# The source lists of a graph kernel: five long gathers and moves by powers of two in place of 49 short gathers

## The chip, the cores and the metric

The kernel runs on one core of a Trainium2 chip. A core has five engines with a queue of instructions each: TensorE (PE), VectorE (DVE), ScalarE (ACT), GpSimd (POOL) and SyncE (SP). Each engine executes its own instructions in the order in which they were issued and waits on semaphores for the others. SP, ACT and POOL also issue DMA transfers. The metric is the time of one execution on the device in microseconds; the median over several executions counts.

## The reference: what is computed

A graph has 6250 nodes with 256 features each and 100000 edges `src -> dst`, sorted by `dst`. Two blocks follow one another, each with a residual and a layer norm:

```python
x = _layernorm(x + _L0_gnn_ref(x, edge_index, Wl1, Wr1, att1, b1, Wl2, Wr2, att2, b2))
x = _layernorm(x + _L1_gnn_ref(x, W, a, src, dst))
```

The first block is two GATv2 layers with 4 heads of 64 channels. Each layer multiplies x by two weight matrices (`xl`, `xr`), and for each edge forms a logit from `leaky_relu(xl[src] + xr[dst])` and the attention vector, takes a softmax of the logits over all edges that end in one node, and adds up `xl[src]` with these weights. The second block is a GAT layer with 8 heads of 32 channels, with logits `s1[src] + s2[dst]`. So each layer needs, for every node, the list of the sources of its edges: a contiguous piece of the array `src`, as the edges are sorted by `dst`.

## The kernel before

The program has a plan (`make_plan`, L715), the three layers (`tile_by_degree`, L1143), and a general path (L81) that runs only if the plan finds that the graph doesn't fit its assumptions (`fits`, `done`).

**The layers.** The nodes are sorted by degree, largest first, and cut into 49 blocks (`NB`) of 128, one node to a partition. A block is worked on with as many columns as its largest node has edges (`cols`; the largest number is `CM` = 38). For each column POOL issues one indirect gather of 128 rows of the table (L1235). VectorE makes the logits (L1504 to L1506), ScalarE the softmax, and TensorE or VectorE adds up.

**The plan** makes what the layers need:

- `near_d`, a table in DRAM with a row for each node: up to 38 source numbers, the rest filled with the number of a node that doesn't exist, and then the node's 256 features;
- `node_i`, which node stands where in the order by degree;
- `xl1_d`, the table of `x @ Wl1` for the first layer, with the place of each node in one more column.

A node n stands at partition n % 128, column n // 128 in the plan's tiles before the change (`part`, L946 to L950). Its steps, in the order of the code:

1. VectorE finds in `dst` where each node's run of edges ends (L927 to L956), and TensorE adds one-hots of these runs into `count`, the degree of each node (L972).
2. Two matmuls give sums over a block's 128 partitions (`pc`, L980, L981); VectorE turns them into `begin_i`, the place in the list where each node's edges begin (L986 to L993).
3. POOL issues 49 indirect gathers (L998): each reads, for 128 nodes, the 38 numbers of the list from the beginning of the node's piece on, into `near`. The list is a copy of `src` in DRAM, `list_d`.
4. VectorE and TensorE work out the place of each node in the order by degree: one-hots `oh` of the degree (L1024), matmuls `pk` and scans into `cum` (L1033 to L1044), `place_f` (L1046); then one-hots `to_hi`, `given`, `to_lo` (L1071 to L1080) and 49 matmuls `pp` (L1085), from which come `node_i` and the check `wrong`, `fits` (L1091 to L1116).
5. `lacking` (L1004) marks in `no` which of a node's 38 columns lie behind its last edge; `fill` (L1011) puts the missing number there with a predicated copy and writes nine columns of nodes to `near_d` from SP's queue (L1016). There are six such spans.

Between these steps stands the making of the first table. `tables(n)` (L848) does the next n of 49 blocks: TensorE turns 128 rows of x (L834) and multiplies them (L843), ScalarE copies the result out of PSUM (L845), SP writes it to `xl1_d` (L846). The blocks are handed out by hand: 12 while VectorE looks for runs, then 1, 2 and 12 between the matmuls of step 4, and 22 behind `pp` (as 4, 7 and 11). The result tiles have ten buffers (`table1_row`). `pk` has two buffers in PSUM and its matmuls come in two groups of three.

The plan is written under `tc.manual_schedule()` (L691), so each engine gets its instructions in the order in which the code issues them. A second such part holds the layers. Between the two all engines read `fits` and branch (L700, L701). POOL begins the layers with small tiles (L1182) and the gathers of `near_d`'s rows for the first three blocks (`start1`, L1595).

Of the kernel before, what the change touches and what calls it, by code (L numbers as in the profile page):

```python
# [26 lines left out]
F32 = mybir.dt.float32  # L27
BF16 = mybir.dt.bfloat16
# [7 lines left out]
P = 128  # L36
# [678 lines left out]
def make_plan(  # L715
# [21 lines left out]

    one = ctx.enter_context(tc.tile_pool(name="plan_one", bufs=1))
# [7 lines left out]
    list_d = dram.tile([-(-E // CM) * CM + CM], I32, name="list_d")  # L746
# [124 lines left out]
    if rest:  # L871
# [9 lines left out]
    nothing = filled_tile("nothing", [1, list_d.shape[0] - E], 0, I32)  # L881
# [3 lines left out]
    nc.scalar.dma_start(list_d[E:].unsqueeze(0), nothing)  # L885
    nc.scalar.dma_start(
        list_d[:E].rearrange("(a b) -> a b", a=a), src.rearrange("(a b) -> a b", a=a)
# [4 lines left out]
    ranks = iota("ranks", [P, CM], [[1, CM]])  # L892
    ones = filled_tile("ones_f", [P, P], 1.0)
# [48 lines left out]
    for what in "lar":  # L942
# [4 lines left out]
    nc.vector.tensor_scalar(  # L947
        part[:, 0, :], run_i, SHIFT, P - 1, op0=OP.logical_shift_right, op1=OP.bitwise_and
    )
    nc.vector.tensor_single_scalar(part[:, 1, :], run_i, SHIFT + 7, op=OP.logical_shift_right)  # L950
# [27 lines left out]

    pc = ps.tile([P, 2, NB], F32, name="pc", tag="ph")
    nc.tensor.matmul(pc[:, 0, :], ones, count, start=True, stop=True)  # L980
    nc.tensor.matmul(pc[:, 1, :], above, count, start=True, stop=True)  # L981
# [3 lines left out]
    block = one.tile([P, NB], F32, name="block")  # L985
    nc.vector.tensor_copy(block, pc[:, 0, :])  # L986
    upto = one.tile([P, NB], F32, name="upto")
    nc.vector.tensor_tensor_scan(upto, ones_k[:, :NB], block, 0.0, op0=OP.mult, op1=OP.add)
    from_f = one.tile([P, NB], F32, name="from_f")
    nc.vector.tensor_sub(from_f, upto, block)  # L990
    nc.vector.tensor_add(from_f, from_f, pc[:, 1, :])
    begin_i = one.tile([P, NB], I32, name="begin_i")
    nc.vector.tensor_scalar(begin_i, from_f, float(E), 0.0, op0=OP.min, op1=OP.max)  # L993
    near = one.tile([P, NB, CM], I32, name="near")
    no = one.tile([P, NB, CM], I32, name="no")
    listed = list_d.rearrange("(a b) -> a b", b=CM)
    for k in range(NB):
        nc.gpsimd.indirect_dma_start(  # L998
            out=near[:, k, :], out_offset=None, in_=listed,
            in_offset=bass.IndirectOffsetOnAxis(ap=begin_i[:, k : k + 1], axis=1),  # L1000
        )
# [136 lines left out]
    for k in spans[4:]:  # L1138
        fill(*k)
# [653 lines left out]
```

## Time and profile before

| what | us |
| --- | --- |
| median of 14 runs (3367.95 to 3373.56) | 3370.39 |
| the profiled execution, its own time | 3369.12 |
| its span, first to last instruction | 3367.3 |
| VectorE busy | 2834.5 (84%) |
| POOL busy | 2464.9 (73%) |
| TensorE busy | 1340.3 (40%) |
| ScalarE busy | 1048.3 (31%) |
| POOL, 49 list gathers L998 | 59.3 |
| POOL, layers' gathers L1235, both tables | 2215.9 (1488.1 + 727.8) |

How to read it: the times of the profile are those of one execution, counted from its first instruction. A busy time is the sum over an engine's instructions; the share is of the span. A line such as `L998 POOL DMA_INDIRECT near<-list_d,begin_i x49 | 59.3, 1211 | 32.1 <-...` gives the line of the code, the engine, the operation, what is written from what, how often, the busy time in us, the mean of one in ns, and how long the engine stood idle just before, with what ended most of that. In a timeline the first two numbers are the start and the duration, and the brackets hold the idle time before and who ended it. An indirect DMA shown on POOL is the time that POOL takes to issue it; the data land later.

### The profile page before, as it was taken

The numbers are of one execution on the slowest core, as the hardware profiler recorded it, in microseconds if no ns is written. First come the engines' busy times: TensorE is split into PE (matmuls) and PEld (weight loads), VectorE is DVE, ScalarE is ACT, GpSimd is POOL, SyncE is SP. The second block draws the span as 40 slices with busy tenths as digits, with TensorE's granted clock in tenths as the row PEclk, the third lists the DMA queues.
The fourth block names the chain that finished last, engine by engine and source line by source line (L and its number), as shares of the span: only waits on it lengthen the run. The fifth ranks groups of instructions, "written<-read, shape, count | busy, mean of one in ns | idle before, by whom it ended". The sixth has DMA issues, their size and how long they took to land.

```text
span 3367.3 us, 23607 instructions
## 1 busy us (share of the span) xinstructions
PE 1340.3 (40%) x5129; PEld 1067.9 (32%) x5130; DVE 2834.5 (84%) x2648; ACT 1048.3 (31%) x4176; POOL 2464.9 (73%) x2613
## 2 busy tenths in 40 slices
PE   6346566666776753445455556563000000000000
PEld 5234445455555543434344444442000000000000
DVE  7289999999999988999999999995977676667666
ACT  3124444444445532444344444442000000000000
POOL 6677777777777777777777777657777777777776
PEclk8677888788888986777777777776555555555555
DMA  9644444444444444444444444434433333333333
GB/s 192 143 112 116 119 117 118 121 120 121 121 120 124 124 131 110 116 118 117 121 120 125 126 131 123 117 97 109 108 108 108 107 108 108 108 108 108 107 107 88
DMA packets 196123, 395.60 MB, mean 117 GB/s; under 512 B 63036, under 2 KB 115514, under 8 KB 195956
## 3 DMA queue, kind: packets, MB, share of 16 engines
q0 software_dynamic: 122048, 338.04, 38.1%
q1 hardware_dynamic: 66226, 54.22, 5.8%
q10 hardware_dynamic: 7698, 1.74, 0.5%
q8 instruction: 45, 0.74, 0.1%
q14 instruction: 106, 0.87, 0.1%
HBM read 353.82 MB, written 40.42 MB: 117 GB/s over the span
## 4 chain that ended last, share of the span: by engine, by line
DVE 30%; POOL 29%; issue 19%; PE 6%; DMA 5%; ACT 4%; DVEq 0%; POOLq 0%; ACTq 0%
POOL g L1235 28%; DVE z L1504 9%; DVE z L1505 8%; DVE lg L1506 8%; PE acc L1418 5%; DMA g<-xl_d,near_r 3%; ACT wt L1381 3%; DVE g L1411 2%; POOL out L1733 1%; DMA g<-whs_d,near_r 1%; DMA out<-y,node_i 1%; DVE weighted L1433 1%; DVE top L1374 1%; PE pm L1362 0%; ACT by L1388 0%
## 5 line engine op out<-in xcount | busy, mean ns | idle before, releaser
L1235 POOL DMA_INDIRECT g<-xl_d,near_r x1569 | 1488.1, 948 | 526.2 <-issue 434.0
L1418 PE MATMUL acc<-g,ident 128*128 128x256 f32 x3408 | 962.6, 452 | 777.3 <-DVE sd L1461 456.2
L1418 PEld LDWEIGHTS acc<-g,ident 128*128 128x128 f32 x3408 | 782.8, 233 | 957.9 <-issue 502.2
L1235 POOL DMA_INDIRECT g<-whs_d,near_r x766 | 727.8, 950 | 233.8 <-issue 227.2
L1504 DVE TENSOR_TENSOR z<-g,pr 128x1820 f32<-128x1820 f32 (+4 forms) x234 | 497.1, 2125 | 16.8 <-DMA g<-xl_d,near_r 8.9
L1505 DVE TENSOR_TENSOR z<-z,at 128x1820 f32<-128x1820 f32 (+4 forms) x234 | 497.5, 2126 | 8.0
L1506 DVE TENSOR_REDUCE lg<-z 128x28 f32<-128x1820 f32 (+4 forms) x234 | 497.3, 2125 | 8.1
L1410 ACT ACTIVATE g<-g,by 128x64 f32<-128x64 f32 x2056 | 500.0, 334 | 0.0
L1411 DVE TENSOR_TENSOR g<-g,wt 128x1792 f32<-128x1792 f32 (+8 forms) x234 | 348.3, 1505 | 2.8
L1442 DVE TENSOR_REDUCE acc_v<-weighted 128x256 f32<-128x4096 f32 (+15 forms) x49 | 343.7, 7014 | 1.7
L1391 ACT ACTIVATE wt<-lg 128x128 f32<-128x128 f32 (+17 forms) x49 | 14.0, 285 | 804.2 <-DVE lg L1390 804.2
L1381 ACT ACTIVATE wt<-lg,top 128x19 f32<-128x19 f32 (+14 forms) x392 | 115.3, 294 | 469.7 <-DVE top L1374 421.6
L1703 DVE TENSOR_TENSOR lg<-g,s_r 128x56 f32<-128x56 f32 (+4 forms) x111 | 22.3, 212 | 269.3 <-DMA g<-whs_d,near_r 215.1
L1433 DVE TENSOR_TENSOR weighted<-g,wt 128x1792 f32<-128x1792 f32 (+4 forms) x111 | 226.6, 2056 | 0.1
L1357 ACT COPY xT<-pt 128x256 f32<-128x256 f32 x147 | 55.0, 374 | 490.3 <-PE pt L1355 490.3
L1362 PE MATMUL pm<-wcat,xT 128*128 128x260 f32 x392 | 99.0, 395 | 22.6 <-ACT xT L1357 22.6
L1362 PEld LDWEIGHTS pm<-wcat,xT 128*128 128x128 f32 x392 | 70.4, 189 | 42.9 <-ACT xT L1357 34.3
L998 POOL DMA_INDIRECT near<-list_d,begin_i x49 | 59.3, 1211 | 32.1 <-DVE begin_i L993 17.4
L1381 ACT ACTIVATION_READ_ACCUMULATOR wt<-lg,top 128x1 f32 x392 | 73.1, 187 | 0.0
L1733 POOL DMA_INDIRECT out<-y,node_i x49 | 49.8, 1017 | 26.1 <-issue 14.2
L1362 PE MATMUL pm<-wh_cat,xT 128*128 128x272 f32 x196 | 59.0, 424 | 22.6 <-ACT xT L1357 22.6
L1362 PE MATMUL pl<-wcat,xT 128*128 128x260 f32 x196 | 57.0, 414 | 25.2 <-ACT xT L1357 25.2
(232 smaller groups left out, 1407.6 us busy)
## 6 DMA issues: line engine op xcount, KB each, us to landing
g<-xl_d,near_r POOLq DMA_INDIRECT x1569, 2.8
g<-whs_d,near_r POOLq DMA_INDIRECT x766, 2.8
whs_d<-row SPq DMA_DIRECT2D x49, 132.0 KB, 2.0
xl_d<-xl SPq DMA_DIRECT2D x49, 130.0 KB, 5.3
xl_d<-row SPq DMA_DIRECT2D x49, 130.0 KB, 2.5
xr_d<-row SPq DMA_DIRECT2D x49, 130.0 KB, 3.0
two<-xl_d SPq DMA_DIRECT2D x49, 130.0 KB, 3.3
two<-xr_d SPq DMA_DIRECT2D x49, 130.0 KB, 3.3
```

The lines of the kernel that those rows point to most:

```text
L1235: nc.gpsimd.indirect_dma_start(out=g[:, j + own - s0, :width], out_offset=None, in_=table, in_offset=source(of, b, j),)
L1362: nc.tensor.matmul(pm, xT[:, c, :], w[:, c, :], start=c == 0, stop=c == 1)
L1381: nc.scalar.activation(wt[:, :, h], lg[:, :S, h], AF.Exp, bias=top[:, h : h + 1], accum_out=den[:, h : h + 1],)
L1410: nc.scalar.mul(g4[:, t, h, :], g4[:, t, h, :], by[:, t - m, h : h + 1])
L1411: nc.vector.tensor_mul(g4[:, :m], g4[:, :m], wt[:, s0 : s0 + m, :].unsqueeze(3).to_broadcast([P, m, H, F // H]),)
L1418: nc.tensor.matmul(acc, ident, g4[:, t], start=s0 + t == 0, stop=s0 + t == S - 1 and not more)
L1433: nc.vector.tensor_mul(prod[:, s0 - base : s1 - base, :].rearrange("p t (h d) -> p t h d", h=H), g[:, :n, :F].rearrange("p t (h d) -> p t ...
L1442: nc.vector.reduce_sum(part, prod[:, : s1 - base, :].rearrange("p s f -> p f s"), axis=AX.X)
L1504: nc.vector.tensor_max(z, g[:, :n, :W2], xr[:, None, :].to_broadcast([P, n, W2]))
L1505: nc.vector.tensor_mul(z, z, at[:, None, :].to_broadcast([P, n, W2]))
L1506: nc.vector.reduce_sum(lg[:, s0:s1, :], z.rearrange("p t (h d) -> p t h d", h=H2), axis=AX.X)
L1733: put = nc.gpsimd.indirect_dma_start(out=out[:, :], out_offset=node(b), in_=y, in_offset=None, bounds_check=N - 1, oob_is_err=False,)
```

## The change

The plan counts its nodes partition by partition: node n now stands at partition n // 49 and column n % 49. So a partition's 49 nodes are neighbours in the sorted edge list, and their sources are one contiguous stretch of it. Each partition reads this stretch in five pieces of 309 numbers (`LONG`), one piece for ten nodes (`STEP`), by five gathers in place of 49. As a node has 16 edges on average (`MEAN`), the piece of node j of ten begins near number 16 j of the piece; how far off it begins (`off`, kept between 0 and 127 by a lead of 64) is known from a running sum over the partition. VectorE takes, for each j, 101 numbers of all five pieces into `moved`, from place 16 j, or from 64 further on where the highest of the seven bits of `off` is set (a copy and a predicated copy). Then it moves all 50 pieces by 32, 16, 8, 4, 2 and 1 numbers where the bit is set, by a predicated copy of the tile onto itself, and the first 38 numbers of each piece are the node's list.

With it go: `begin_i` now comes from sums over a row and a prefix over the partitions, so the two matmuls `pc` have one column; the division by 49 is a multiplication and a shift; `oh` and the bits stand on VectorE ahead of the moves, the scans `cum` behind them; all six `fill`s are issued together behind `lacking`, where two, one, one and two stood apart before; `near_d` and the place column of `xl1_d` are written in the other order; the check has a term more. The order of the `tables` calls is as before.

```diff
+    SEGS, STEP, BITS = 5, 10, 7
+    LEAD = 1 << BITS - 1
+    MEAN = E // N
+    LONG = MEAN * (STEP - 1) + CM + 2 * LEAD - 1
+    WIDE = CM + LEAD - 1
...
+    nc.scalar.dma_start(list_d[:LEAD].unsqueeze(0), nothing[:, :LEAD])
+    nc.scalar.dma_start(list_d[LEAD + E :].unsqueeze(0), nothing)
...
-    nc.vector.tensor_scalar(
-        part[:, 0, :], run_i, SHIFT, P - 1, op0=OP.logical_shift_right, op1=OP.bitwise_and
+    nc.vector.tensor_single_scalar(part[:, 1, :], run_i, SHIFT, op=OP.logical_shift_right)
+    nc.vector.tensor_single_scalar(part[:, 0, :], part[:, 1, :], float(by), op=OP.mult)
+    nc.vector.tensor_single_scalar(part[:, 0, :], part[:, 0, :], down, op=OP.logical_shift_right)
+    nc.vector.scalar_tensor_tensor(
+        part[:, 1, :], part[:, 0, :], -float(NB), part[:, 1, :], op0=OP.mult, op1=OP.add
     )
-    nc.vector.tensor_single_scalar(part[:, 1, :], run_i, SHIFT + 7, op=OP.logical_shift_right)
...
-    pc = ps.tile([P, 2, NB], F32, name="pc", tag="ph")
-    nc.tensor.matmul(pc[:, 0, :], ones, count, start=True, stop=True)
-    nc.tensor.matmul(pc[:, 1, :], above, count, start=True, stop=True)
+    total = one.tile([P, 1], F32, name="total")
+    nc.vector.reduce_sum(total, count, axis=AX.X)
+    pc = ps.tile([P, 2], F32, name="pc", tag="ph")
+    nc.tensor.matmul(pc[:, 1:], above, total, start=True, stop=True)
+    nc.tensor.matmul(pc[:, :1], ones, total, start=True, stop=True)
+    upto = one.tile([P, NB], F32, name="upto")
+    nc.vector.tensor_tensor_scan(upto, ones_k[:, :NB], count, 0.0, op0=OP.mult, op1=OP.add)
...
+    begin_i = one.tile([P, SEGS], I32, name="begin_i")
+    nc.vector.tensor_scalar(begin_i, begin_f, float(E), 0.0, op0=OP.min, op1=OP.max)
+    piece_of = one.tile([P, SEGS, LONG], I32, name="piece_of")
+    listed = list_d.rearrange("(a b) -> a b", b=LONG)
+    for k in range(SEGS):
+        nc.gpsimd.indirect_dma_start(
+            out=piece_of[:, k, :], out_offset=None, in_=listed,
+            in_offset=bass.IndirectOffsetOnAxis(ap=begin_i[:, k : k + 1], axis=1),
+        )
...
+    oh = one.tile([P, KEYS, NB], BF16, name="oh")
+    nc.vector.tensor_tensor(
+        oh, steps, key[:, None, :].to_broadcast([P, KEYS, NB]), op=OP.is_equal
+    )
...
+    off_i = one.tile([P, SEGS, STEP], I32, name="off_i")
+    nc.vector.tensor_scalar(off_i, off, 0.0, float(2 * LEAD - 1), op0=OP.max, op1=OP.min)
+    bit = one.tile([P, BITS, SEGS, STEP], I32, name="bit")
+    for k in range(BITS):
+        nc.vector.tensor_scalar(
+            bit[:, k], off_i, k, 1, op0=OP.logical_shift_right, op1=OP.bitwise_and
+        )
+    moved = one.tile([P, SEGS, STEP, WIDE], I32, name="moved")
+    for k in range(STEP):
+        for first_at in (0, LEAD):
+            data = piece_of[:, :, MEAN * k + first_at : MEAN * k + first_at + WIDE]
+            if first_at == 0:
+                nc.vector.tensor_copy(moved[:, :, k, :], data)
+            else:
+                nc.vector.copy_predicated(
+                    moved[:, :, k, :],
+                    bit[:, BITS - 1, :, k : k + 1].to_broadcast([P, SEGS, WIDE]), data,
+                )
+    every = moved.rearrange("p s j w -> p (s j) w")
+    bits = bit.rearrange("p b s j -> p b (s j)")
+    for k in range(BITS - 2, -1, -1):
+        n = CM + (1 << k) - 1
+        nc.vector.copy_predicated(
+            every[:, :, :n], bits[:, k, :].unsqueeze(2).to_broadcast([P, SEGS * STEP, n]),
+            every[:, :, 1 << k : (1 << k) + n],
+        )
+    near = every[:, :NB, :CM]
...
-    for k in range(NB):
-        nc.gpsimd.indirect_dma_start(
-            out=near[:, k, :], out_offset=None, in_=listed,
-            in_offset=bass.IndirectOffsetOnAxis(ap=begin_i[:, k : k + 1], axis=1),
-        )
...
-            near_d[k0 * P : k1 * P, :CM].rearrange("(k p) c -> p k c", p=P).bitcast(I32),
+            near_d.rearrange("(p k) c -> p k c", k=NB)[:, k0:k1, :CM].bitcast(I32),
...
     tables(1)
-    oh = one.tile([P, KEYS, NB], BF16, name="oh")
...
-            xl1_d[:NP, W2:].rearrange("(b p) w -> p b w", p=P), place_f.unsqueeze(2)
+            xl1_d[:NP, W2:].rearrange("(p b) w -> p b w", b=NB), place_f.unsqueeze(2)
...
     for k in spans:
         lacking(*k)
-    fill(*spans[0])
-    fill(*spans[1])
+    for k in spans:
+        fill(*k)
...
-        node_i, got[:, 1, :], float(P), got[:, 0, :], op0=OP.mult, op1=OP.add
+        node_i, got[:, 0, :], float(NB), got[:, 1, :], op0=OP.mult, op1=OP.add
...
-    fill(*spans[2])
...
     tables(7)
-    fill(*spans[3])
...
     tables(NB)
-    for k in spans[4:]:
-        fill(*k)
```

## The prediction

> **What bounds the kernel now.** I read the page first, for where the changed code lies. All of it is in `make_plan`, before the three attention layers. The later part, 3237 of the 3367 us, is not edited: POOL issues one gather every 1.25 us there and VectorE is nearly always busy. So the question is by how much the first gather of that part moves.
>
> ```profile
> span 3367.3 us, 23607 instructions
> ...
> L998 POOL DMA_INDIRECT near<-list_d,begin_i x49 | 59.3, 1211 | 32.1 <-DVE begin_i L993 17.4
> ...
> L1235 POOL DMA_INDIRECT g<-xl_d,near_r x1569 | 1488.1, 948 | 526.2 <-issue 434.0
> ```
>
> Second, the timeline of POOL over the plan: the 49 list gathers run from 40.2 to 114.3 us, and the first gather of the layers starts at 130.6.
>
> ```profile
> 40.23 1.36 POOL L998 DMA_INDIRECT near<-list_d,begin_i  x1 [17.41 <-DVE begin_i L993]
> 41.89 0.95 POOL L998 DMA_INDIRECT near<-list_d,begin_i  x1 [0.30 <-issue]
> ...
> 113.33 0.94 POOL L998 DMA_INDIRECT near<-list_d,begin_i  x1 [0.30 <-issue]
> 129.82 0.24 POOL L1182 IOTA numbers<- 128x128 f32 x1 [15.54 <-DMA near_d<-near]
> 130.02 0.12 POOL L1186 IOTA own_number<- 128x1 f32 x1
> 130.10 0.19 POOL L1200 MEMSET ones_l<- 128x128 f32 x1
> 130.59 0.97 POOL L1595 DMA_INDIRECT near_r<-near_d,node_i  x1 [0.30 <-issue]
> ```
>
> Third, the waits between 70 and 131 us (engine, line, what it waited for: us in total, times, longest). VectorE waits 38.4 us for list gathers, so it has room there. But ScalarE, which copies the table blocks out of PSUM, also waits: 14.3 us for table writes.
>
> ```profile
> DVE near L1013 <- DMA near<-list_d,begin_i: 38.4, 5, 15.5
> POOL numbers L1182 <- DMA near_d<-near: 15.5, 1, 15.5
> ACT xl L845 <- DMA xl_d<-xl: 14.3, 5, 8.4
> ACT xT L836 <- PE pt L834: 13.7, 1, 13.7
> ```
>
> Fourth, the timelines of VectorE, TensorE and ScalarE. They show a second chain as long as POOL's: scans, one-hots, `pp`, then 22 table blocks, the last of which is copied out at 117.4 us, as late as the last fill.
>
> ```profile
> 39.85 0.72 DVE L1024 TENSOR_TENSOR oh<-steps_k,key_b 128x1078 bf16<-128x1078 bf16 x1
> 41.13 1.22 DVE L1034 TENSOR_TENSOR_SCAN cum<-ones_k,pk 128x512 f32<-128x512 f32 x1 [0.55 <-PE pk L1033]
> ...
> 61.39 6.68 DVE L1080 TENSOR_TENSOR to_lo<-each_lo,to 128x6272 bf16<-128x6272 bf16 x1
> ...
> 116.31 0.55 DVE L1013 COPY_PREDICATED near<-no,far 128x342 int32<-128x342 int32 x1 [15.47 <-DMA near<-list_d,begin_i]
> 117.12 0.33 DVE L1013 COPY_PREDICATED near<-no,far 128x152 int32<-128x152 int32 x1 [0.25 <-DMA near<-list_d,begin_i]
> ```
> ```profile
> 42.40 0.18 PE L1033 MATMUL pk<-oh,ones_b 128*128 128x54 bf16 x1 [1.31 <-DVE cum L1034]
> ...
> 68.13 4.99 PE L1085 MATMUL pp<-given,to_lo 128*128 128x147 bf16 x49 [8.85 <-DVE to_lo L1080]
> ```
> ```profile
> 116.98 0.38 ACT L845 COPY xl<-pm 128x260 f32<-128x260 f32 x1 [8.40 <-DMA xl_d<-xl]
> ```
>
> Two chains therefore end together. Taking only POOL's away can win nothing unless the table chain also ends earlier. The change makes it later.
>
> **The change part by part.** *Gathers.* 49 become five. The row sums, the one-column matmuls and the scan in front take the place of instructions of 0.2 to 0.3 us each, so I leave `begin_i` at 40.0 us (+0.5 at most, from two more instructions on `part` and one on `count`). POOL then issues at 40.2: 1.36 + 0.30, three of 1.25 and 0.95, so the fifth is out at 46.6. Landing takes 2.8 us by the layers' row gathers (1044 bytes a row, near the 1236 here) and 5.7 us by the median of the list gathers issued between 40 and 60 us. I take 4: the pieces are there at 50.6 (49.4 to 52.3).
>
> *The moves.* In the built order VectorE does key, `oh`, `off` and seven `bit` instructions first (some 3 us, in the shadow of the gathers), then ten pairs of a copy and a predicated copy of 505 numbers, then six predicated copies of 50 times 69, 53, 45, 41, 39 and 38. No other work is placed between the wait for the gathers and these. A predicated copy takes 0.546 us for 342 numbers and 0.333 for 152, so 0.163 us and 1.12 ns a number. That makes 0.73 for 505 and 17.0 for the six (14250 numbers). A plain copy of 505 int32 is not in the trace. The one-source row (128x256 f32 in 0.286, 128x128 in 0.23) gives 0.40, the two-source rows (0.416 for 256, 2.05 for 1820) give 0.68; one source is the nearer, I take 0.45. With 0.03 between dependent instructions: 10 x (0.48 + 0.76) + 17.0 + 0.2 = 29.6 us, bounds 28 and 32. If copying with a repeated mask or onto itself is dearer, no row shows it.
>
> [...]
>
> The moves end at 50.6 + 29.6 = 80.2 us.
>
> *Who waits.* `cum`, which began at 41.1, now stands behind them on VectorE. The third `pk` matmul needs the first scan, because `pk` has two buffers, so TensorE stops at about 43 us, and behind it in order stand 14 table blocks, `pp` and the last 22 blocks. TensorE's and ScalarE's 38 us of stop are not hidden: TensorE has nothing else. From `cum` to the end of `to_lo` took 26.9 us (41.1 to 68.1) and `pp` ended 5.1 later. Both are unedited: 80.2 + 26.9 + 5.1 = 112.2 for the end of `pp`, against 73.1. That is 39 us late. The 14 middle blocks (1.10 us each) fit inside, and so does `place_f`'s write of 6272 numbers, 16.7 us to landing. Its address order changes from strided to consecutive; I price that at nothing, since nothing behind it ends the stage.
>
> *The last 22 blocks.* Before: 117.4 - 73.1 = 44.3 us. Of that 22 x 1.10 = 24.2 is the pace of a block, 14.3 the waits on table writes, and 5.8 the weights of layer two on ScalarE and the start. The write waits shrink in part: SP stood still before `fill` of the third and fourth span (from 86 to 93 us) with table writes behind it. Now all six fills are issued before those blocks, and their 6272 short rows, once spread from 77 to 122 us, share the DMA queues with the first table writes. Ends 0 and 14.3; I take 5, since ten row buffers cover 11 us of delay. 35.0 us: the last block is copied out at 147.2.
>
> *The tail.* Before: 13.2 us from the last copy (117.4) to the first gather of the layers, because two fills were issued behind the last writes (7.0 us to landing). Now table writes come last: up to 2 us of SP backlog, 5.9 to landing, 0.8 for POOL's three small instructions. I take 8.7 (7 to 13.2). First gather: 155.9, against 130.6, so **+25.3 us**.
>
> *The rest.* The six fills lose their waits, 3.1 us of work stays in the chain beside `pp`. The check gains two instructions of 0.2 us in the shadow of four blocks. The start gains one issue on ScalarE's queue (0.5 us) beside its 1.2 us of idle time before the first block. Equal-degree nodes come in another order, so the layers read other rows; each gather still costs POOL 0.95 us, and I put this at 0, -3 to +3.
>
> **Sum.** The profiled execution took 3369.1 us, 1.3 below the median of the 14 runs (3370.4). 3369.1 + 25.3 = 3394.4; against the median 3395.7. I write 3395. Low end: pieces at 49.4, moves 28, no write waits, tail 7: pp ends at 109.4, first gather at 146.4, +15.8. High end: 52.3, 32, 14.3, 13.2: 173.8, +43.2.
>
> **The rivals.** *Pile-up of transfers* (0.12): the fills, 22 table writes, three blocks of x and the layer weights come at once behind 112 us. From 73 to 118 us the DMA engines were 91% busy, so a pile-up is possible; the idle stretch from 50 to 80 us, when no tables are made, speaks against more. Price: all 14.3 of waits and 13.2 of tail, +39, 3409.
>
> *A small loss* (0.10): ScalarE's 5.8 us halves because the weights' products are ready earlier, no write waits, short landing: +13, 3383. Against it: the fills in front.
>
> *Faster* (0.05): the new node order shortens the layers' waits for rows. The chain that ended last holds 3% of the span in landings of `g<-xl_d`, 101 us. To decide, a third of it (32 us) would have to go: 3363 or less. For it: the order of rows does change. Against it: sources are drawn at random in either numbering. The plan itself can't end earlier: for that `pp` must end by 86 us, so the moves would have to take 4 us.
>
> *It doesn't do what it says* (0.01): if a running sum left the window of 128, the whole general path would run as well, thousands of us. From the inputs the offsets lie between 19 and 97 and the largest degree is 32, so it does not.
>
> **How the numbers follow.** The forecast (+16 to +34) has 0.68, with 0.04 left for a loss that all but vanishes. Range: 3381 to 3411 leaves out the ends of both rivals. Two tenths of a per cent, 6.7 us, is about what a measurement here tells from no change. Faster 0.05, same 0.04, slower 0.91.
>
> **What would show it.** Five POOL gathers ending near 47 us; sixteen predicated copies and ten copies filling VectorE from about 50 to 80; TensorE silent from 43 to 80; `pp` ending near 112; the last table copy near 147; the first `near_r` gather near 156. The prediction fails if the predicated copies run at two numbers a cycle (-12 us), if the layers' part is not 3237 us long, or if the table blocks no longer stand behind `pp`.

## The result, and the profile after

The changed kernel takes 3409.95 us (median of 6 runs, 3409.39 to 3414.31) where the kernel before took 3369.75 in the same comparison (28 runs): 1.0122 times as long, with a 95% interval of 1.0112 to 1.0131. It is slower by 40 us; the forecast was 25 us, and 3410 lies just below the upper end of the range.

The profiled execution of the changed kernel took 3410.9 us. From its page, the span and two groups (busy us, mean ns, then idle time before and what ended it):

```profile
span 3409.1 us, 23560 instructions
...
L1293 POOL DMA_INDIRECT g<-xl_d,near_r x1569 | 1487.5, 948 | 527.9 <-issue 432.5
...
L1240 POOL IOTA numbers<- 128x128 f32 x1 | 0.2, 243 | 105.2 <-DMA near_d<-xt 105.2
```

The row gathers of the layers cost what they cost before (1488.1 and 526.2 of idle time there). POOL now stands idle for 105.2 us in the plan, after its five gathers. Its timeline (start, us, instruction, and in brackets the idle time before):

```profile
40.50 1.15 POOL L1016 DMA_INDIRECT piece_of<-list_d,begin_i  x1 [17.24 <-DVE key_b L1021]
...
45.71 0.95 POOL L1016 DMA_INDIRECT piece_of<-list_d,begin_i  x1 [0.30 <-issue]
151.84 0.24 POOL L1240 IOTA numbers<- 128x128 f32 x1 [105.19 <-DMA near_d<-xt]
...
164.75 0.97 POOL L1653 DMA_INDIRECT near_r<-near_d,node_i  x1 [12.43 <-DMA xl_d<-xl]
```

The gathers end at 46.7 us instead of 114.3, and yet the first gather of lists for the layers comes at 164.75 instead of 130.59, 34.2 us later. What POOL waits for last is a table write (`xl_d<-xl`). VectorE shows why the tables are late:

```profile
51.35 0.48 DVE L1045 COPY moved<-piece_of 128x505 int32<-128x505 int32 x1 [8.44 <-DMA piece_of<-list_d,begin_i]
51.87 0.74 DVE L1047 COPY_PREDICATED moved<-bit,piece_of 128x505 int32<-128x505 int32 x1
...
62.72 17.88 DVE L1055 COPY_PREDICATED moved<-bit,moved 128x3450 int32<-128x3450 int32 x6
80.50 1.20 DVE L1089 TENSOR_TENSOR_SCAN cum<-ones_k,pk 128x512 f32<-128x512 f32 x1
```

It moves numbers from 51.35 to 80.5 us, and the first scan `cum`, at 41.1 before, stands behind that. The waits between 36 and 185 us (engine, line, what it waited for: total, times, longest) name the two that follow from it:

```profile
POOL numbers L1240 <- DMA near_d<-xt: 105.2, 1, 105.2
...
PE pk L1088 <- DVE cum L1089: 39.5, 1, 39.5
...
ACT xl L859 <- DMA xl_d<-xl: 17.1, 5, 7.4
```

TensorE stands for 39.5 us before the third `pk`, with table blocks and `pp` behind it; before, this wait was 1.3 us. After `pp`, ScalarE waits 17.1 us for table writes, which is more than the 14.3 of before, though the list gathers that ran beside the tables are gone. SP's timeline has the place where this begins:

```profile
115.18 0.32 SPq L1117 DMA_DIRECT2D near_d<-x_end  x1
115.55 0.28 SPq L1118 DMA_DIRECT2D next_e<-in_dst  x1
115.94 1.80 SPq L1122 DMA_DIRECT2D xl_d<-nobody  x1
118.23 9.27 SPq L1075 DMA_DIRECT2D near_d<-moved  x6
127.59 1.74 SPq L829 DMA_DIRECT2D xt<-in_x  x1
129.43 3.40 SPq L860 DMA_DIRECT2D xl_d<-xl  x2
```

The six writes of lists keep SP from 118.2 to 127.5 us, and the first table write behind `pp` goes out at 129.4. The last table block is copied out at 159.2:

```profile
139.91 0.38 ACT L859 COPY xl<-pm 128x260 f32<-128x260 f32 x1 [7.44 <-DMA xl_d<-xl]
...
158.82 0.38 ACT L859 COPY xl<-pm 128x260 f32<-128x260 f32 x1 [3.02 <-DMA xl_d<-xl]
```

From there on everything is shifted. The first row gather comes 34.8 us later than before (169.17 against 134.36), the last scatter of the output ends 35.5 later (3397.6 against 3362.1). The other order of the nodes costs the layers 0.7 us from the first row gather to the last scatter, 1.3 us counted from the first gather of lists. At the very end 6.3 us more are lost: from the last scatter to the end of the program it takes 11.5 us, and took 5.2. In the trace's records (no view of the profile lists them) that is POOL's INC_SWDGE_SEM (1.72 us against 0.49) and its last DRAIN (6.35 against 1.29). 34.2 + 1.3 + 6.3 = 41.8, the difference of the two spans.

The experiments ran later, on three chips, on which the kernel before takes 3869 to 3884 us. On the one of them where it was run again, the changed kernel takes only 1.0017 times as long (1.0000 to 1.0034). So times are compared with the kernel before of the same chip only, and the times in microseconds that the expectations name, worked out for 3370 us, can't be held against these runs; the places in the plan can. The changed kernel's plan runs there as in the first runs (first gather of lists at 166.5 against 164.75), so places in it are compared across chips; the kernel before is another matter, which its own run there shows.

### The profile page after: what moved, and what is told of

Its sections match the earlier page's. It is cut to its first block, busy times and chain, and to the rows that moved or that the text cites. A ratio compares the mean times of both kernels' runs of the same rounds, so it can differ in the third digit from the quotient of the medians.

```text
span 3409.1 us, 23560 instructions
## 1 busy us (share of the span) xinstructions
PE 1351.6 (40%) x5129; PEld 1076.6 (32%) x5130; DVE 2866.0 (84%) x2690; ACT 1048.5 (31%) x4176; POOL 2410.5 (71%) x2570
## 4 chain that ended last, share of the span: by engine, by line
POOL 32%; DVE 27%; issue 20%; DMA 7%; PE 5%; ACT 4%; DVEq 0%; POOLq 0%; ACTq 0%
POOL g L1293 31%; DVE z L1562 8%; DVE z L1563 8%; DVE lg L1564 8%; PE acc L1476 4%; DMA g<-xl_d,near_r 4%; ACT wt L1439 3%; DVE g L1469 2%; POOL out L1791 1%; DMA xl_d<-xl 1%; DMA out<-y,node_i 1%; DMA g<-whs_d,near_r 1%; DVE top L1432 1%; ACT g L1468 0%; DMA near_r<-near_d,node_i 0%
## 5 line engine op out<-in xcount | busy, mean ns | idle before, releaser
L1240 POOL IOTA numbers<- 128x128 f32 x1 | 0.2, 243 | 105.2 <-DMA near_d<-xt 105.2
L1420 PE MATMUL pl<-wcat,xT 128*128 128x260 f32 x196 | 57.2, 415 | 25.2 <-ACT xT L1415 25.2
```

The costliest lines, as they stand in the source:

```text
L1420: nc.tensor.matmul(pm, xT[:, c, :], w[:, c, :], start=c == 0, stop=c == 1)
```

## The experiments

### The moves behind the check

Theory: the moves cost what the chain scans, `pp`, tables is held up by. Rival: the lists and tables are late because the transfers pile up, wherever the moves stand. The copies and shifts move as they are, from ahead of the scans to behind the check and the weights of layer two; the six `fill`s go behind the last table. So two things change place, the moves and the lists' writes.

```diff
-    for k in range(STEP):
-        for first_at in (0, LEAD):
...
-    for k in range(BITS - 2, -1, -1):
...
     near = every[:, :NB, :CM]
...
-    for k in spans:
-        fill(*k)
     got = one.tile([P, 3, NB], F32, name="got")
...
     left(1, nc.vector)
     right(1)
+    for k in range(STEP):
+        for first_at in (0, LEAD):
...
+    for k in range(BITS - 2, -1, -1):
...
     tables(NB)
+    for k in spans:
+        fill(*k)
```

> Order alone: the same 26 copying instructions, but behind the check and the weights on VectorE, and the six fills behind the last table block. Chain theory (the loss comes from what waits behind the moves on VectorE and TensorE): pp ends at 75 us (73 before, 115 in the changed kernel), the last table block is copied out at 113 to 120, the fills follow and land some 16 us later, the first gather of the layers starts at 133 to 140, the time is 3375 to 3386. Pile-up theory (the loss comes from all transfers of the late stage lying close together): the fills still come together, so no more than 10 to 15 us are won, 3395 to 3400.

Measured: 3853.48 us, 0.9957 of the kernel before (0.9938 to 0.9976). `pp` ends at 75.9 us, the last table block is copied out at 108.8, and the first gather of lists comes at 135.7. From its waits, and the timelines of VectorE, ScalarE, SP and POOL:

```profile
POOL numbers L1240 <- DMA near_d<-moved: 88.6, 1, 88.6
...
ACT xl L859 <- DMA xl_d<-xl: 0.9, 1, 0.9
```
```profile
97.71 18.07 DVE L1176 COPY_PREDICATED moved<-bit,moved 128x3450 int32<-128x3450 int32 x6
```
```profile
108.46 0.38 ACT L859 COPY xl<-pm 128x260 f32<-128x260 f32 x1 [0.92 <-DMA xl_d<-xl]
```
```profile
116.42 9.56 SPq L1059 DMA_DIRECT2D near_d<-moved  x6
```
```profile
135.71 0.97 POOL L1653 DMA_INDIRECT near_r<-near_d,node_i  x1 [0.23 <-issue]
```

The same moves now stand beside the tables instead of ahead of them, and 31 us come back (166.5 to 135.7), where the rival allowed 10 to 15. The theory of the chain holds for `pp` and the first gather; the last table block came even earlier than its 113 to 120. As the lists' writes moved too, this run alone doesn't separate the two; the next leaves the writes where they are. The 22 blocks behind `pp` take 32.9 us here, with 0.9 us of waiting for table writes: without lists among them, they are that much faster than the 44.0 of the changed kernel. And the lists' writes are now the last to land: POOL waits for `near_d<-moved`.

### The shifts left out

This kernel leaves out the six predicated copies of the tile onto itself, so its lists aren't the graph's; all other instructions stay.

```diff
-    for k in range(BITS - 2, -1, -1):
-        n = CM + (1 << k) - 1
-        nc.vector.copy_predicated(
-            every[:, :, :n], bits[:, k, :].unsqueeze(2).to_broadcast([P, SEGS * STEP, n]),
-            every[:, :, 1 << k : (1 << k) + n],
-        )
```

> Leaves out the six predicated copies of the tile onto itself (17.9 us in the changed kernel), so the lists begin up to 63 places off. Chain theory: the scans start at 62.7 and everything behind moves up by 17.9 us, first gather of the layers at 147, time 3392. If something else than the moves held the late stage (the writes of lists and places in their new address order, or the row buffers), part of it is kept: a gain of 0 to 10 us, 3400 to 3410.

Measured: 3863.25 us, 0.9982 of the kernel before (0.9957 to 1.0006). The scans begin at 62.2 us, and the first gather comes at 147.7, 18.9 us ahead of the changed kernel. TensorE and POOL:

```profile
63.47 0.20 PE L1082 MATMUL pk<-oh,ones_b 128*128 128x54 bf16 x1 [20.67 <-DVE cum L1083]
```
```profile
147.67 0.97 POOL L1647 DMA_INDIRECT near_r<-near_d,node_i  x1 [11.64 <-DMA near_d<-xt]
```

17.9 us of instructions on VectorE are worth 18.9 us at the end: here a microsecond ahead of the scans goes about one for one into the chain.

### The lists' writes apart, and at the old addresses

These two ask why ScalarE waits as long as before. Together the 6272 short rows (152 bytes) take the DMA engines 21.7 us of all 16 in the changed kernel, a mean of 55 ns for a packet; in the kernel before it is 28 ns (both means worked out from the DMA records of the trace, over all packets of 152 bytes; the 26 in the expectations is a little low). Either the writes slow each other when they come at once, or their new order of addresses does.

```diff
-    for k in spans:
-        fill(*k)
+    fill(*spans[0])
+    fill(*spans[1])
...
     right(1)
+    fill(*spans[2])
...
     tables(7)
+    fill(*spans[3])
...
     tables(NB)
+    for k in spans[4:]:
+        fill(*k)
```

> The six fills at the four places they had before (two, one, one, two). If their coming together makes the table writes wait, ScalarE's 17.1 us of waits for table writes fall below 10, the 152-byte rows take about 26 ns each as before in place of 55, but the two last fills stand behind the last table writes and the tail grows from 5.5 towards 13: time 3400 to 3412. If the new address order of the rows is what makes them slow, 55 ns a row and the waits stay, and the time is 3408 to 3418.

Measured: 3882.33 us, 1.0040 of the kernel before (1.0021 to 1.0059). SP's timeline, ScalarE's wait and POOL:

```profile
118.60 1.03 SPq L1075 DMA_DIRECT2D near_d<-moved  x2
...
127.39 0.37 SPq L1075 DMA_DIRECT2D near_d<-moved  x1
...
140.43 0.59 SPq L1075 DMA_DIRECT2D near_d<-moved  x1
...
157.32 2.23 SPq L1075 DMA_DIRECT2D near_d<-moved  x2
```
```profile
ACT xl L859 <- DMA xl_d<-xl: 10.2, 5, 5.2
```
```profile
166.32 0.24 POOL L1244 IOTA numbers<- 128x128 f32 x1 [119.36 <-DMA near_d<-moved]
167.10 0.97 POOL L1657 DMA_INDIRECT near_r<-near_d,node_i  x1 [0.29 <-issue]
```

A packet takes 31.5 ns, ScalarE waits 10.2 us instead of 17.1 (the expectation for writes that hold each other up was below 10), and the 22 blocks take 39.1 us. But the first gather comes no earlier (167.1), because the last two writes of lists now land last. What the blocks win, the tail gives back: 13.8 us from the last copy to the first gather, against 5.6.

The other kernel writes all six together, but to the addresses of the kernel before; the lists then stand in other nodes' rows, the general path runs as well, and only its plan can be read.

```diff
-            near_d.rearrange("(p k) c -> p k c", k=NB)[:, k0:k1, :CM].bitcast(I32),
+            near_d[k0 * P : k1 * P, :CM].rearrange("(k p) c -> p k c", p=P).bitcast(I32),
```

> The fills write their rows to the addresses they had before (row k x 128 + p in place of p x 49 + k), so a node's list stands in another node's row; nothing else is changed. If the address order makes the rows slow: 26 ns in place of 55 a row, the waits of ScalarE for table writes fall by 8 to 12 us and the time to 3398 to 3402. If the order of addresses does not matter: within 2 us of 3410.

Measured: 13639.59 us. In its plan a packet takes 55 ns, ScalarE waits 17.0 us, the last block is copied at 160.5 and the first gather comes at 166.0: all as in the changed kernel. So it isn't the addresses. Nor is it table writes beside them: in the changed kernel no packet of a table write moves between 117 and 135 us, while the lists are written, and with the moves behind the check a packet takes 55 ns as well, the slowest there, 70 to 79 ns in stretches of 5 us, behind the last table write. It builds up: of the changed kernel's packets the first 881 take 14 ns, those of the next stretches of 5 us 45, 76 and 89. Six writes at once is what all seven traces at 55 to 59 ns have in common; the four below with two times three writes lie at 43 to 48. What in the memory or the queues makes it so, no run here shows.

### The end of the program: 44 gathers more, and skipped rows together

The 6.3 us at the end were not in any forecast. Two theories: the DRAIN depends on the number of indirect DMAs (2559 before, 2515 after), or on the rows that the last scatter skips (22 nodes that don't exist, neighbours before and scattered after).

The changed kernel itself, on the chip of these two:

> The changed kernel itself, so that the three kernels beside it have it on the same chip. Both theories of the end expect the first gather of lists at 164 to 167 us, a last DRAIN of POOL of 6.3 to 6.4 us (6.36 in the changed kernel's trace, 1.29 in the one before), and, if the chip runs the layers like the first one, a ratio to the kernel before of 1.011 to 1.013.

Measured: 3882.97 us, 1.0017 of the kernel before (1.0000 to 1.0034); first gather of lists at 166.5, DRAIN 6.35 us. End and plan are as in the first runs; the ratio is not.

```diff
+    spare = one.tile([P, NB - SEGS, 16], I32, name="spare")
+    short = list_d[: list_d.shape[0] // 16 * 16].rearrange("(a b) -> a b", b=16)
+    for k in range(NB - SEGS):
+        nc.gpsimd.indirect_dma_start(
+            out=spare[:, k, :], out_offset=None, in_=short,
+            in_offset=bass.IndirectOffsetOnAxis(ap=begin_i[:, :1], axis=1),
+        )
```

> Beside the changed kernel: 44 small gathers more on POOL right after the five, so that the program again issues 2559 indirect DMAs, as the kernel before (the changed kernel: 2515). Nobody reads what they gather; POOL is idle there for 105 us. Theory C1, POOL's last DRAIN depends on how many indirect DMAs the program issued: the DRAIN falls from 6.36 to about 1.3 us, INC_SWDGE_SEM from 1.72 to about 0.5, and the program is about 6 us shorter than the changed kernel, 0 to 2 us of which the gathers may give back by taking DMA time from the pieces and tables. Theory C2, the DRAIN depends on the skipped rows of the last scatter: 6.3 to 6.4 us as before, and no change of the time beyond 2 us.

Measured: 3886.57 us, 1.0017 of the kernel before (0.9996 to 1.0039); DRAIN 1.29 us, INC_SWDGE_SEM 0.49, first gather of lists at 172.5. The end is that of the kernel before again. The time isn't shorter, since the gathers beside the tables cost the plan 6.0 us, about what the end gives back.

```diff
-    KEYS = high - low + 1
+    KEYS = high - low + 2
...
     nc.vector.tensor_scalar(key, key, -1.0, float(high), op0=OP.mult, op1=OP.add)
+    nc.vector.scalar_tensor_tensor(key, count, 0.0, key, op0=OP.is_equal, op1=OP.add)
```

> Beside the changed kernel: the 22 nodes that do not exist get a class of their own behind the others, so that the last scatter skips 22 neighbouring partitions, as in the kernel before, and not 22 scattered ones. It costs one VectorE instruction of 128x49 more (about 0.2 us) and 49 columns more in the scans and sums (about 0.3 us). Theory C1 (number of indirect DMAs): DRAIN 6.3 to 6.4 us, time within 1 us of the changed kernel. Theory C2 (skipped rows): DRAIN about 1.3 us, about 5 to 6 us shorter.

Measured: 3883.48 us, 1.0026 of the kernel before (1.0001 to 1.0050); DRAIN 6.35 us. The skipped rows have nothing to do with it.

### The moves right behind the places

The chain suggests a version: scans and `pp` first, then the moves in two halves beside the tables, plain copies on ScalarE, and the lists' writes among the last table writes. `placed` makes the ten predicated copies, `shifted` the six shifts of the nodes from the first to the second number.

```diff
+    def plain():
+        for k in range(STEP):
+            nc.scalar.copy(moved[:, :, k, :], piece_of[:, :, MEAN * k : MEAN * k + WIDE])
...
     tables(12)
+    plain()
     nc.vector.tensor_mul(cum, cum, ohf)
...
-    for k in spans:
+    placed()
+    shifted(0, 27)
+    tables(13)
+    for k in spans[:3]:
+        fill(*k)
+        tables(1)
+    shifted(27, SEGS * STEP)
+    tables(5)
+    for k in spans[3:]:
         fill(*k)
+        tables(0)
     got = one.tile([P, 3, NB], F32, name="got")
...
-    tables(4)
+    tables(NB)
...
```

> A version meant to beat both: scans, sums and places run ahead of the moves; the ten plain copies go to ScalarE (10 of about 0.6 us, from when the pieces have landed); VectorE makes the ten predicated copies (7.3 us) and the shifts in two halves (about 9.3 and 8.7 us) right after the places are handed to TensorE, with half of the lists filled and written between the halves; SP has the writes of the lists among the last table writes; the check comes behind the moves. From the trace of the kernel with the moves behind the check: places handed over at 71, lists marked at 73.3, then 7.3 + 9.3 + 1.3 + 8.7 + 1.3 = 28 us, so the last list is written at 101 to 103, tables end by 105 (97 without the wait for the check, some more for the lists' packets), the check by 110. Theory of the chain: first gather of lists at 109 to 118 us, 13 to 21 us ahead of the kernel before (130.6) and 18 to 27 ahead of the kernel with the moves behind (135.7); POOL's last DRAIN still 6.3 us, so 3352 to 3364 us against 3370 on a chip like the first, 0.995 to 0.998. Rival: the lists' packets in the stretch of table writes (55 ns each where six writes come together) hold the tables up as they did in the changed kernel: tables end at 115 to 120, first gather at 121 to 127, and the time is that of the kernel before within 4 us.

Measured: 3847.29 us, 0.9928 of the kernel before (0.9898 to 0.9957). The plain copies on ScalarE take 0.62 us each, the lists are moved by 99.9, the last table block is copied at 101.1, and the first gather of lists comes at 124.0, later than the theory had it (109 to 118) and where the rival had it (121 to 127). But the rival's reason, tables held up to 115 or 120, did not come. VectorE, SP and POOL:

```profile
77.93 10.39 DVE L1060 COPY_PREDICATED moved<-bit,moved 128x1863 int32<-128x1863 int32 x6
...
89.70 8.95 DVE L1060 COPY_PREDICATED moved<-bit,moved 128x1587 int32<-128x1587 int32 x6
```
```profile
110.04 5.38 SPq L1082 DMA_DIRECT2D near_d<-moved  x3
```
```profile
123.23 0.24 POOL L1255 IOTA numbers<- 128x128 f32 x1 [76.81 <-DMA wh_cat<-in_L_gnn_W]
123.95 0.97 POOL L1668 DMA_INDIRECT near_r<-near_d,node_i  x1 [0.23 <-issue]
```

No engine is late any more, SP is: the last three lists stand behind the table writes till 110, and behind them come the loads of weights that POOL waits for.

### Those loads early, with and without small gathers

Two changes: the loads of weights and biases go out ahead of the first scans, and 44 gathers of 8 partitions follow the five, to bring the number of indirect DMAs back to 2559.

```diff
     tables(12)
+    for c in range(2):
+        nc.sync.dma_start(
+            wh[:, c, :F].rearrange("p (h d) -> p h d", h=H1),
+            w3[:, c * P : (c + 1) * P, :].rearrange("h p d -> p h d"),
+        )
...
+    for k in range(NB - SEGS):
+        nc.gpsimd.indirect_dma_start(
+            out=spare[:8, k, :], out_offset=None, in_=short,
+            in_offset=bass.IndirectOffsetOnAxis(ap=begin_i[:8, :1], axis=1),
+        )
```

> The version with the moves right behind the places, with two changes. Its loads of the last layer's weights and of the biases (two and four DMAs on SP) go out before the first scans, where SP and the DMA engines have room, instead of behind the lists; and 44 small gathers of 8 partitions x 16 numbers follow the five on POOL, so that the program again issues 2559 indirect DMAs. Theory of the chain: the first gather of lists, which waited for those weights till 123.2 us while the last list was written at 115.5, comes at 116 to 120. Theory C1 (POOL's last DRAIN goes by the number of indirect DMAs, as the kernel with 44 full gathers showed): DRAIN 1.3 us. A rival for the end: it goes by the descriptors moved (122048 packets on that queue before, 120720 in the changed kernel, and some 5600 more with 44 full gathers); 44 gathers of 8 partitions add only about 350, and the DRAIN stays at 6.3. Both as the chain and C1 have it: 0.988 to 0.993 of the kernel before on a chip that runs it in about 3870 us, 0.993 to 0.996 on one that runs it in 3370.

Measured: 3865.51 us, 0.9954 of the kernel before (0.9937 to 0.9971). None of its expectations came. The last table block is copied at 119.5 and the first gather comes at 131.3; the DRAIN takes 8.72 us, neither the 1.3 of one theory nor the 6.3 of the other. With 2559 indirect DMAs it is 1.29 or 8.72, so the theory of their number, which the run with 44 full gathers seemed to have shown, falls.

The same without the 44 gathers, and then with 8 full ones:

> The version with the moves right behind the places and the loads of weights and biases early, without the 44 small gathers. In the run with them the last table copy ended at 119.5 us, without them (loads late, another chip) at 101.1. Theory: the gathers that POOL issues beside the tables held the tables up; then the last table copy ends at 99 to 104 here, the first gather of lists comes at 114 to 120 (131.3 with the gathers; 124.0 with the loads late), and the time is 0.987 to 0.993 of the kernel before on a chip that runs it in about 3880 us, 0.993 to 0.998 on one that runs it in 3370. Rival: that chip was slower by itself in this stretch; then the tables end at 112 or later and the first gather comes after 124. POOL's last DRAIN 6.35 us as in all programs with the five gathers alone.

> The same with 8 full gathers (128 partitions x 16 numbers) behind the five. The last DRAIN of POOL was 1.29 us with 2559 indirect DMAs that name all 128 partitions (the kernel before; the changed kernel with 44 full ones more), 8.72 with 2559 of which 44 name 8 partitions, 6.35 with 2515. So the number of DMAs doesn't set it. If it grows with the rows named, from 6.35 by 2.37 us for the 352 rows of those 44, then 1024 rows more give 13.2 us, or less where it starts anew in between; if it goes by whether the small gathers are there, it is 6.35 again. The plan is the other's within 2 us.

Measured: 3842.96 us, 0.9920 of the kernel before (0.9903 to 0.9937), and 3856.12 (one run). Last table block at 106.7 and 106.8, first gather at 127.3 and 130.1, DRAIN 6.35 and 7.00 us. For the eight gathers the expectation had 13.2 or 6.35, and a plan within 2 us of the other's; it is 2.8 us later. The ends of ScalarE's tables with and without the small gathers:

```profile
119.11 0.38 ACT L859 COPY xl<-pm 128x260 f32<-128x260 f32 x1 [2.11 <-PE pb L1212]
```
```profile
106.36 0.38 ACT L859 COPY xl<-pm 128x260 f32<-128x260 f32 x1 [0.50 <-PE pm L857]
```
```profile
ACT xl L859 <- DMA xl_d<-xl: 7.1, 4, 4.3
```

The number for the tables without small gathers (99 to 104) was too early and that of the rival (112 or later) too late; the first gather came where the rival had it, after 124. 12.7 us of the difference went with the gathers (and another chip), and 5.6 us to the kernel with the loads late are left, which the chip or the early loads may have made. In this version ScalarE waits 7.1 us for table writes and POOL at last for one. The early loads brought nothing that shows: 0.9920 and 0.9928 agree within their intervals.

The end of the program, from the records of all traces but that with the old addresses, where the general path adds gathers:

| indirect DMAs | INC_SWDGE_SEM, us | last DRAIN, us |
| --- | --- | --- |
| 2559, the kernel before (both traces) | 0.49 | 1.29 |
| 2515, the five gathers alone (seven kernels) | 1.72 | 6.35 |
| 2515 and 8 full | 1.89 | 7.00 |
| 2515 and 44 of 8 partitions | 2.31 | 8.72 |
| 2515 and 44 full | 0.49 | 1.29 |

The two programs that were traced on two chips have the same end on both. Eight full gathers add 0.65 us to the DRAIN, 44 of 8 partitions add 2.37, and 44 full ones take 5.06 away: neither the number of DMAs nor that of the rows goes with it alone. What it counts stays open.

### The kernel before on one of the later chips

> The kernel before, unchanged, for its trace on the same chip: the later chips run it in about 3870 us where the first one took 3370, and the changed kernel is only 1.0017 of it there. If the plan is the same on all chips, the first gather of lists comes at 129 to 133 us and the first row gather at 133 to 137; what then differs from 1.0122 lies in the layers, whose time from the first row gather to the last scatter is 10 to 35 us longer for the kernel before than for the changed kernel.

Measured: 3889.07 us (one run; median of the 14 beside it 3883.88). Its plan isn't the same there: the first gather of lists comes at 156.2 us, not at 129 to 133. The waits between 36 and 165 us:

```profile
POOL numbers L1182 <- DMA near_d<-near: 40.6, 1, 40.6
DVE many L1114 <- issue: 28.1, 1, 28.1
PEld pm L843 <- remote: 22.7, 1, 22.7
PE pm L843 <- remote: 22.3, 1, 22.3
...
ACT xl L845 <- remote: 19.3, 3, 9.4
```

Between 82 and 120 us VectorE (28.1 us), TensorE (22.3) and, in three pieces, ScalarE (19.3) stand without a releaser that the profile can name ("issue" and "remote"), while POOL goes on issuing its gathers every 1.25 us. The changed kernel has five gathers there and comes 1.8 us later on these chips, the kernel before 25.6 us.

That makes most of the other ratio: 23.8 of the 29.5 us by which the changed kernel loses less there (10.7 us against 40.2). Each kernel's first gather of lists, and its median less that of the kernel before on the same chip:

| kernel | first gather, us | to the kernel before, us | the first less the second |
| --- | --- | --- | --- |
| moves at the places | 124.0 | -25.0 | 149.0 |
| the same, loads early | 127.3 | -29.7 | 157.0 |
| the same, small gathers | 131.3 | -18.4 | 149.7 |
| moves behind the check | 135.7 | -15.7 | 151.4 |
| shifts left out | 147.7 | -5.9 | 153.6 |
| the changed kernel | 166.5 | +10.7 | 155.8 |
| lists' writes apart | 167.1 | +13.2 | 153.9 |
| skipped rows together | 167.7 | +11.2 | 156.5 |
| 44 full gathers more | 172.5 | +14.3 | 158.2 |

The last column would be the first gather of the kernel before, if nothing else differed. Its mean is 154, and the trace says 156.2. So over nine kernels the time goes by the first gather, about one for one within some 5 us. The ends of the program, up to 9 us apart, are left in; with them taken out the column runs from 155 to 163, 160 on average. From the medians, 10.7 - 10.3 (of the first gathers) - 6.3 (of the ends) leaves -6 us for the layers of the changed kernel there. Single traces would say -30 us, but those two runs lie 5 us above and 7 us below their medians.

Why the three engines stand there isn't settled. The 44 small gathers went with a table stage 12 us longer on another chip, the 44 full ones with 5 us on the same chip, which fits the gathers as a cause. But on the first chip the same 49 gathers ran without these waits, so by themselves they are not enough; a run of the kernel before without them, on such a chip, was not made.

## Why the prediction was right, and where it was short

| step | forecast | measured |
| --- | --- | --- |
| fifth gather issued | 46.6 | 46.7 |
| pieces there | 50.6 | 51.35 |
| moves on VectorE | 29.6 | 29.2 |
| scans begin | 80.2 | 80.5 |
| `pp` ends | 112.2 | 115.2 |
| last 22 table blocks | 35.0 | 44.0 |
| of it waits for table writes | 5 | 17.1 |
| last copy to first gather | 8.7 | 5.6 |
| first gather of lists, later by | 25.3 | 34.2 |
| layers | 0 | 1.3 |
| end of the program | not considered | 6.3 |

**The mechanism was right.** Two chains ended together before; the change shortens POOL's and puts 29 us at the head of the other. The runs with the moves behind the check (31 us back, with the lists' writes moved too) and without shifts (18.9 us back, all else in place) show this, not only the trace.

**The moves were priced well.** A predicated copy of 505 takes 0.73 to 0.74 us (forecast 0.73), a plain one 0.46 to 0.48 (0.45), the six shifts 17.9 (17.0 and the gaps); neither the repeated mask nor the copy onto itself is dearer than the rows of the kernel before. For the sixteen predicated copies the trace has 25.2 us (ten of 0.73 and 17.9) where the line through the rows of the kernel before gives 24.2. The low end of the range took 28 us for all the moves, a figure that no run shows: they took 29.2 here, and 29.5 behind the check. Nor does a run show the twofold rate that the prediction names as a way to fail: a predicated copy of 505 took 0.73 to 0.75 us in both.

**`pp` ended 3.0 us later than the sum.** 0.3 is from the moves, 0.3 from `pp` itself, and 2.4 from VectorE's wait for the second group of `pk` (3.35 us, 0.97 before); two table blocks stand ahead of that group on TensorE, which had just been idle for 39 us. The profile shows what the sum left out: the granted TensorE clock is 0.50 from 80 to 86 us and 1.00 from 88 to 102, and the four matmuls of such a block take 1.94 us at 0.50; before, at 41 to 50 us, the clock was 1.00 and they took 1.04. From the timelines of TensorE, after and before:

```profile
82.30 1.94 PE L857 MATMUL pm<-wcat,xT 128*128 128x260 f32 x4
...
109.80 5.39 PE L1140 MATMUL pp<-given,to_lo 128*128 128x147 bf16 x49 [8.79 <-DVE to_lo L1135]
```
```profile
42.75 1.04 PE L843 MATMUL pm<-wcat,xT 128*128 128x260 f32 x4
```

**The term that failed** is "the write waits shrink in part", 5 us with ends at 0 and 14.3. It measured 17.1, beyond the upper end. The reason given for less was that the lists are issued ahead of the blocks; that is just what made it worse. Six writes of short rows at once take 55 ns a packet where the kernel before had 28, SP is held by them for 9.3 us with the table writes behind it, and the runs at 31.5 ns (apart) and 55 ns (old addresses) show that being together costs, and not the addresses: written apart the blocks take 4.9 us less. Whether the slower packets or SP's being held costs more, no run separates. The old 14.3 had stood beside the 49 gathers and four writes of lists; 32.9, 39.1 and 44.0 us for the same 22 blocks, with no lists, four writes apart and six together, is the price list that was missing. The rival "pile-up of transfers" had this price, 3409, at a chance of 0.12; its other half, a long tail, did not come, and the end of the program filled the gap.

**The tail** was 3.1 us shorter than forecast: no list is written behind the tables, and the last writes found little backlog. That is a piece of luck for the range: the tail cancels what `pp` lost, and with a tail of 8.7 us the time would by this estimate have been 3413, above its upper end.

**The end of the program** was in no term. No row of the trace of before would have shown it, but it was assumed without a word that nothing behind the layers depends on the plan. From the first gather of lists to the end it is 3244 us, not the 3237 that the prediction named as a sign of being right.

**The rivals.** "Faster", by another order of nodes in the layers, fell: it moved them by 1.3 us in the first runs. "It doesn't do what it says" fell too. The small loss wanted no write waits, and there were more.

## What to carry to other kernels

Ask of a new piece of work on an engine what stands behind it on that engine: the same 29 us of moves cost 31 us more ahead of the scans than behind the check (with the lists' writes moved along). When waits for writes are priced, bound them by how the writes will be packed and not by what they were; here the same bytes cost the DMA engines twice the time when six writes came at once (55 ns a packet against 28). And compare the whole chain up to the first instruction of the unedited part: it explained nine kernels to within 5 us.

The best version here, with the moves behind the places, is 0.992 of the kernel before (0.9903 to 0.9937) on one of the later chips. Where the kernel before takes 3370 us it was not run; its first gather (127.3) would stand against 130.6 there, and its end is 6.3 us longer, so by this estimate it would win next to nothing.

## What the runs showed of the hardware that was not expected

- Writes of 152 bytes to DRAM took 28 ns a packet when six DMAs were spread over 49 us (26 on a later chip, over 72 us), 31.5 ns spread over 44 us in the changed order, and 55 to 59 ns when they were issued together, whether in the old or the new order of addresses.
- POOL's last DRAIN took 1.29, 6.35, 7.00 or 8.72 us, the same on two chips for the two programs traced twice; the number of indirect DMAs alone doesn't decide it.
- In the later runs the kernel before took 500 us more than in the first, and in its plan the three compute engines waited for 19 to 28 us without a visible releaser while POOL went on issuing gathers.
- TensorE's granted clock was 0.50 from 80 to 86 us, behind 39 us without work, and also from 36 to 42 us, ahead of them; four matmuls of a table block took 1.94 us at 0.50 and 1.04 at 1.00.
